# Product 3 of the result in seven block products, batches 2 to 5

## The chip, the core and the metric

The kernel runs on one core of a Trainium2 chip. The metric is the device time in microseconds (us) of one execution. Its engines run side by side, each through its own list of instructions in order: TensorE (PE; PEld is its weight load), VectorE (DVE), ScalarE (ACT) and GpSimd (POOL). Transfers (DMA) are issued from the lists of SyncE (SP) and of POOL; those that add to what lies at their target are issued from POOL. TensorE writes into eight banks of PSUM of 128 x 512 float32 each; VectorE and ScalarE bring results from there to SBUF.

## What is computed

Cross attention over eight batches in float32, `x` and `ctx` of 512 channels and 1024 positions each:

```python
q = einsum('bcn,dc->bnd', x1, Wq) + bq          # d = 64
k = einsum('bcn,dc->bdn', x2, Wk) + bk[:, None]
v = einsum('bcn,dc->bdn', x2, Wv) + bv[:, None]
attn = softmax(einsum('bnd,bdm->bnm', q, k), axis=2)
out = einsum('bcm,bnm->bcn', v, attn) + x1
```

## The kernel before

The value weights are applied last: first y = x2 times the exponentials, then the result o = Wv times y, divided by the sums and with bv and x1 added. Both matrix products are made by a scheme of seven products of half-size blocks in place of eight (numbered 1 to 7 in the table MULT), with sums of blocks on the left and on the right (S1 to S4, T1 to T4) that VectorE makes. The results run through chains: product 1 alone, 1+6, 1+6+5 and so on are grown in the same PSUM bank, and copied out where two results part.

Many of the seven are themselves made in seven block products of 256 columns ("inner" products; `inner_product`, L591). For the result, a block product is one matmul of 128 x 128 by 128 x 256, since its inner blocks have one slice of 128; a plain product of two slices and two rows of blocks is four matmuls of 512 columns.

`period(s, n, nn, nnn)` (L1154) writes out the order by hand for the end of batch s and the start of batch n = s + 1, whose scores and exponentials are made while s is finished. `s.six` is true for batches 2 to 5: in these, product 6 of y is an inner one too. The end of a period is what matters here:

- `multiply_57` (L714) makes products 5, 7 and 3 of the result. 5 and 3 are plain and grow in the bank pair a (after 1 and 6); 7 is an inner one in the pair c. ScalarE's copies of its chain and two exponentials of batch n stand between (the hooks). `complete` adds the third part to the second bank on VectorE.
- `evict_o(s, "22")` reads the pair c, then `second(4)` grows product 4 in it, and `evict_o(s, "21")` reads it again.
- `evict_o(s, "12")` copies the pair a with the bias into the tile r12 (tag "r", ScalarE). Its transfers, x1 added from DRAM and the result written, are kept as `n.leave` and issued in the next period, after `complete_1`.
- Between them POOL issues `sum_t3` (two transfers that add e tiles), `add_11(n, "S3")`, and `total_0(n)`: a VectorE sum over the blocks of the exponentials of half 0, an all-reduce over the partitions, and a small transfer "fews" that lays the sums over partitions.
- The next period (s and n move up by one) makes products 1, 2 and 6 of y, with `total_1` (sum 1 on VectorE, its all-reduce on POOL), `evict_y(s, "11")` from the pair c, `invert(s, 0)` (VectorE adds and inverts fews) and then the left sums of product 7 from S3. The scores of the next batch use the pair c for their second tile.

Tiles share SBUF by tags: a tile waits until its tag's last holder has been read for the last time (with bufs=2, the holder before that). The tag "fold" holds maxima and sums, with two buffers; "y22" holds y22 and, in batches 2 to 5, the copy u1 of product 1 of y; "aI3" holds block sums.

Batch 7 (`multiply_573`, L631) makes product 3 in seven block products already, with 5, 7 and 4, in an order of its own; its left sums of w_S4 are made in its period (`left_values("o3", "S4")`, L1505). In batches 0 and 1 sum 0 of batch 1 is made by three adding transfers (`add_tile`) onto a copied tile (`copy_first`).

Of the kernel before, what the change touches and what calls it, by code (L numbers as in the profile page):

```python
# [15 lines left out]
def kernel(  # L16
# [48 lines left out]
    P = 128  # L65
# [211 lines left out]

    def total_0(s):

        s.mx[0] = f = sb.tile([P, 2, H], F32, tag="fold", name=f"sum_{s.b}_0", bufs=2)  # L280
        x, y = (s.inner[i, "m"].rearrange("q z k (p f) -> q z k p f", p=D) for i in (1, 2))
        nc.vector.tensor_tensor(f.rearrange("q k (p z f) -> q z k p f", p=D, z=2), x, y, ALU.add)
        fold_halves(s, 0, ALU.add)
        s.den[0] = sb.tile([P, H], F32, tag="den", name=f"den_{s.b}_0", bufs=2)
        nc.gpsimd.partition_all_reduce(s.den[0], f[:, 0, :], P, ReduceOp.add)  # L285
        s.few[0] = sb.tile([D, 2, H // P], F32, tag="fews", name=f"fews_{s.b}", bufs=2)
        nc.gpsimd.dma_start(
            s.few[0].rearrange("p z f -> p (z f)"), s.den[0][0:1, :].rearrange("o (p f) -> o p f", p=D)
        )

    def sum_1(s):

        t = s.t["T3"]
        s.mx[1] = sb.tile([P, 2, H], F32, tag="fold", name=f"sum_{s.b}_1", bufs=2)
        nc.vector.tensor_tensor(s.mx[1], t[:, 0:2, :], t[:, 2:4, :], ALU.add)
        fold_halves(s, 1, ALU.add)

# [12 lines left out]
    def invert(s, h):  # L310

        few = s.few[h]
        s.row[h] = row = dram.tile([1, H], F32, tag="row", name=f"row_{s.b}_{h}")
        to = row.rearrange("o (p f) -> (o p) f", p=P)
        if h == 0 and s.b > 1:
            nc.vector.tensor_tensor(few[:, 0, :], few[:, 0, :], few[:, 1, :], ALU.add)
# [296 lines left out]
    def left_values(i, k):  # L613

        x = w[k]
        inner_w[i] = v = {f"{p + 1}{q + 1}": x[:, q : q + 1, ts(p, P)] for p in range(2) for q in range(2)}
        if i == "o3":
            sums = sb.tile([P, 4, 1, P], F32, tag="aS1", name=f"w_I{k}")
        else:
            sums = const.tile([P, 4, 1, P], F32, name=f"w_I{k}")  # L620
# [10 lines left out]
    def multiply_573(s):  # L631
# [33 lines left out]
        for x in ORDER573:  # L665
# [15 lines left out]
            elif x[0] == 4:  # L681
                part, k = divmod(x[1], 2)
                if x[1] == 2:
                    s.bank["last"] = last = ps_a.tile([P, H], F32, tag="c0", name="ps_last")
                if x[1] == 0:
                    last_left(s, True)
                    evict_o(s, "12", rows=(0,))
                ps, j, n = ((a[0], 0, slice(0, H)), (last, 1, left), (a[1], 1, right))[part]
                nc.tensor.matmul(
                    ps[:, n],  # L690
                    w["22"][:, k, ts(j, P)],
                    s.y["T4"][:, k, n],
                    start=part == 1 and k == 0,
                    stop=k == 1,
                    skip_group_check=True,
                )
            else:
                i, z = f"o{x[0]}", x[1]
                ps, opens, copies = steps[x]
                inner_product(s, i, z, ps, opens)  # L700
                for o, of in copies:
                    copy(o, of)
                if x == (7, 7):
                    add_v("22", v7)
                    add_v("21", v7)
                elif x == (3, 1):
                    add_v("12", v3)
                elif x == (7, 3):
                    evict_o(s, "22")
                elif x == (3, 5):  # L710
                    evict_o(s, "12", rows=(1,))
                    last_left(s)

    def multiply_57(s, hook):  # L714

# [233 lines left out]
    def evict_o(s, k, hook=None, rows=range(2)):  # L949
# [18 lines left out]
        if add is None:  # L968
            o = sb.tile([P, 2, H], F32, tag="u1" if k == "11" else "r", name=f"r{k}_{s.b}")
            for j in range(2):  # L970
                nc.scalar.activation(o[:, j, :], s.bank[bank, j], AF.Identity, bias=bias(j))  # L971
                if hook:
                    hook(j)
        else:
            u = s.tmp[add]
            o = sb.tile([P, 2, H], F32, tag="y12", name=f"o{k}_{s.b}") if k == "21" else u
# [32 lines left out]
    def copy_first(s, h):  # L1009

        s.mx[h] = sb.tile([P, 2, H], F32, tag="fold", name=f"sum_{s.b}_{h}", bufs=2)
        nc.scalar.copy(s.mx[h], s.e[h][:, :, 0, :])

    def sums(s, h):
        for i in range(1, MH):
            fold(s, h, i, "sum", ALU.add)
        total(s, h)

    def head_queries(s, x_sb, h, n, bank=None):

# [31 lines left out]
    def head(s):  # L1052
# [36 lines left out]
        s.mx[0] = f = sb.tile([P, 2, H], F32, tag="fold", name=f"max_{s.b}_0", bufs=2)  # L1089
# [64 lines left out]
    def period(s, n, nn, nnn):  # L1154
# [278 lines left out]
                sum_y(s, "T1")  # L1433
        hooks = {}
        if s.b == 0:
            hooks = {6: lambda: exponential(n, 0, 1), 4: lambda: copy_first(n, 0)}
# [31 lines left out]
        if five:  # L1468
            if nn is None:
                scale_y(s, "22")  # L1470
            sum_y(s, "T1")
            weave(
                in_turn(lowers(n, 0, 2 + s.six, MH), lowers(n, 1, 0, 2)),
                sums_o7,
            )
        if s.b == 0:
            add_tile(n, 0, 1)
            sum_y(s, "T4")
        if n is None:
            sum_y(s, "T4")  # L1480
# [3 lines left out]
        if s.b == 0:  # L1484
            exponentials(n, 0, 2)
            lower(n, 0, 3)
            add_tile(n, 0, 2)
# [13 lines left out]
        else:  # L1501
            nc.gpsimd.dma_start(s.x[:, 2:4, 0:H], s.tmp[6], accum_op=ALU.add)
        second(2)
        if n is None:
            weave(left_values("o3", "S4"))  # L1505
        evict_o(s, "11", while_11 if n else None)
        if s.b == 0:
            add_tile(n, 0, 3)
            add_x1(s, "21")
        if n:  # L1510
            if five:
# [43 lines left out]
        if n:  # L1555
# [6 lines left out]
                left_stream(n, 2, n.a["12"], "aI3" if n.b > 1 else "aS4"),  # L1562
            )
            last = evict_o(s, "12")
            if five:
                negate(n, "S3")
                add_11(n, "S3")
            n.leave = [last] if five else [leave, last]
            second(4)
            if five:  # L1570
                total_0(n)
            else:
                total(n, 0)
            evict_o(s, "21")
        else:
            finish(s)
# [43 lines left out]
```

## Time and profile before

| | us |
|---|---|
| median of three runs | 665.11 (664.92 to 665.66) |
| the profiled execution | 665.49 |
| its span from first to last instruction | 663.5 |
| TensorE busy, share of the span | 658.6, 99% |
| VectorE busy | 625.3, 94% |
| ScalarE busy | 379.0, 57% |
| POOL busy | 208.9, 31% |

The profile is of one execution. A row of the timeline gives start, duration, engine, line, operation, `out<-in` by the program's names (batch numbers left out), shapes and count, and in brackets the idle time ahead of it and what ended it. Rows of the list of waits give total, times and longest. Rows of transfers give count, size and the time from issue to landing. Line numbers are those of the kernel before unless said otherwise.

### The profile page before, as it was taken

What the parts mean: (1) busy time and instruction counts of PE and PEld (TensorE: products, weight loads), DVE (VectorE), ACT (ScalarE), POOL (GpSimd) and SP (SyncE); (2) the same over time, 40 slices, a digit from 0 to 9 for tenths busy, and PEclk for the clock granted to TensorE, in tenths of its full rate; (3) what the DMA queues carried; (4) which work ended last, traced back from release to release, by engine and by line L of the source; (5) the groups of instructions that cost most, each with busy time, mean ns of one, the idle gap of its engine ahead of it and who ended that gap; (6) DMA issues with size and microseconds to landing.
All of it is one profiled execution on the core that took longest, in us unless ns stands there. A gap on an engine that the chain in (4) does not pass through costs nothing.

```text
span 663.5 us, 8006 instructions
## 1 busy us (share of the span) xinstructions
PE 658.6 (99%) x2626; PEld 434.2 (65%) x2626; DVE 625.3 (94%) x890; ACT 379.0 (57%) x727; POOL 208.9 (31%) x179
## 2 busy tenths in 40 slices
PE   9999999999999999999999999999999999999997
PEld 5435755756658666677666686576865757666865
DVE  1999999999999999999999999999999999999997
ACT  3755457446475575665766646756567446474332
POOL 0125215631335402363034430354212640224300
PEclk9999999999999999999999999999999999999999
DMA  8687578994789759897598895987928995368614
GB/s 326 261 271 256 124 250 150 212 259 144 261 170 223 190 161 282 177 232 192 145 285 175 206 239 161 250 178 182 277 50 197 217 204 175 78 128 183 121 40 150
DMA packets 47368, 129.05 MB, mean 195 GB/s; under 512 B 5472, under 2 KB 5984, under 8 KB 47328
## 3 DMA queue, kind: packets, MB, share of 16 engines
q0 software_dynamic: 20336, 55.12, 45.8%
q1 hardware_dynamic: 26848, 73.29, 30.4%
q8 instruction: 21, 0.34, 0.2%
q14 instruction: 19, 0.16, 0.1%
q10 hardware_dynamic: 144, 0.14, 0.1%
HBM read 87.83 MB, written 16.81 MB: 158 GB/s over the span
## 4 chain that ended last, share of the span: by engine, by line
PE 94%; DVE 5%; issue 1%; ACT 0%
PE ps_yc L596 9%; PE ps_ya L596 7%; PE ps_oc L485 7%; PE ps_oa L730 6%; PE ps_s L236 6%; PE ps_ya L485 4%; PE ps_q L191 4%; PE ps_oa L485 4%; PE ps_i5chain L596 3%; PE ps_k L191 3%; PE ps_i7chain L596 3%; PE ps_i4b L881 3%; PE ps_i1chain L596 3%; PE ps_i2chain L596 3%; PE ps_i3chain L596 3%; PE ps_oc L881 2%
## 5 line engine op out<-in xcount | busy, mean ns | idle before, releaser
L340 DVE TENSOR_TENSOR e<-e,top 128x1024 f32<-128x1024 f32 x60 | 72.1, 1217 | 0.2 <-POOL top L272 0.2
L349 ACT ACTIVATE e<-e 128x1024 f32<-128x1024 f32 x60 | 62.8, 1058 | 15.9 <-DVE e L340 15.5
L272 POOL PARTITION_ALL_REDUCE top<-max x16 | 32.1, 2008 | 103.6 <-DVE max L266 44.2
L245 ACT COPY e<-ps_s 128x512 f32<-128x512 f32 x90 | 47.7, 619 | 10.2 <-PE ps_s L236 10.2
L304 POOL PARTITION_ALL_REDUCE den<-sum x10 | 33.4, 3337 | 43.2 <-DVE sum L266 38.3
L236 PE MATMUL ps_s<-q,k 64*128 64x512 f32 (+1 forms) x188 | 46.6, 598 | 0.0
L256 DVE TENSOR_TENSOR max<-max,e 128x1024 f32<-128x1024 f32 x30 | 36.5, 1218 | 0.3
L236 PEld LDWEIGHTS ps_s<-q,k 64*128 64x128 f32 x188 | 17.5, 186 | 19.9 <-issue 16.9
L916 DVE TENSOR_TENSOR y<-y,den 128x1024 f32<-128x1024 f32 x24 | 29.2, 1220 | 0.3
L787 ACT COPY ps_yc<-ps_i7chain 128x256 f32<-128x256 f32 x32 | 11.4, 357 | 30.2 <-PE ps_i7chain L596 25.6
L787 ACT COPY ps_ya<-ps_i1chain 128x256 f32<-128x256 f32 x28 | 10.0, 357 | 31.6 <-PE ps_i1chain L596 28.1
L730 PE MATMUL ps_oa<-yT,w_S 128*128 128x512 f32 x56 | 27.5, 592 | 0.0
L285 POOL PARTITION_ALL_REDUCE den<-sum x6 | 19.4, 3229 | 25.3 <-DVE sum L266 25.3
L730 PE MATMUL ps_oa<-y,w_S 128*128 128x512 f32 x56 | 26.3, 592 | 0.0
L325 POOL DMA_DIRECT2D den<-row x12 | 6.7, 561 | 60.0 <-DMA row<-few 36.6
L191 PE MATMUL ps_q<-x_in_x_dram,wqk_sb 128*64 128x512 f32 x112 | 25.6, 598 | 0.0
L485 PE MATMUL ps_oc<-yT,w 128*128 128x512 f32 x56 | 25.3, 594 | 0.1
L787 ACT COPY ps_ya<-ps_i5chain 128x256 f32<-128x256 f32 x32 | 11.5, 360 | 24.1 <-PE ps_i5chain L596 20.0
L485 PE MATMUL ps_oa<-yT,w_S 128*128 128x512 f32 x56 | 25.2, 593 | 0.0
L550 DVE TENSOR_TENSOR aI<-a 128x256 f32<-128x256 f32 x60 | 24.7, 411 | 0.0
L596 PE MATMUL ps_yc<-e,aI 128*128 128x256 f32 x92 | 23.6, 379 | 0.0
L983 POOL DMA_DIRECT2D r<-in_x_dram x14 | 18.3, 1309 | 15.9 <-ACT r L971 15.9
(358 smaller groups left out, 1861.3 us busy)
## 6 DMA issues: line engine op xcount, KB each, us to landing
x_in_x_dram<-in_x_dram SPq DMA_DIRECT2D x60, 512.0 KB, 7.5
a<-in_x2T_dram SPq DMA_DIRECT2D x32, 512.0 KB, 5.7
aS<-in_x2T_dram POOLq DMA_DIRECT2D x21, 512.0 KB, 5.7
eT<-eT POOLq DMA_DIRECT2D x16, 512.0 KB, 11.8
r<-in_x_dram POOLq DMA_DIRECT2D x14, 512.0 KB, 7.1
uo<-in_x_dram POOLq DMA_DIRECT2D x14, 512.0 KB, 8.8
out_dram<-r SPq DMA_DIRECT2D x14, 512.0 KB, 3.3
e<-e POOLq DMA_DIRECT2D x13, 512.0 KB, 7.1
```

The costliest lines, as they stand in the source:

```text
L191: nc.tensor.matmul(ps[r, :], w_sb[:, c, :], s.x[:, c, ts(h, H)], start=(c == 0), stop=(c == CT - 1),)
L236: nc.tensor.matmul(ps[g][:, n], s.k[r, ts(i, P)], s.q[r, ts(h, H)][:, n], start=True, stop=True)
L245: nc.scalar.copy(e[:, g, i, :], ps[g])
L256: nc.vector.tensor_tensor(f, e[:, :, 0, :] if i == 1 else f, e[:, :, i, :], op)
L304: nc.gpsimd.partition_all_reduce(s.den[h], s.mx[h][:, 0, :], P, ReduceOp.add)
L340: nc.vector.tensor_tensor(e, e, top, ALU.subtract)
L349: nc.scalar.activation(e, e, AF.Exp)
L485: nc.tensor.matmul(ps, left[ka][:, k, ts(j, P)], right[kb][:, k, :], start=opens and k == 0, stop=i in (2, 3, 4) and k == n_k - 1, skip_gr ...
L596: nc.tensor.matmul(ps, s.inner[i][ka][:, k, :], s.inner[i, "t"][kb][:, k, :], start=opens and k == 0, stop=z in (2, 3, 4) and k == n_k - 1 ...
L730: nc.tensor.matmul(ps, w[ka][:, k, ts(j, P)], s.y[kb][:, k, :], start=False, stop=i == 3 and k == 1, skip_group_check=True,)
L787: nc.scalar.copy(out, of)
L881: nc.tensor.matmul(ps, s.inner[i][ka][:, k, :], s.inner[i, "t"][kb][:, k, :], start=opens and k == 0, stop=z in (2, 3, 4) and k == n_k - 1 ...
```

## The change

In batches 2 to 5 `multiply_all_573` takes the place of `multiply_57`: product 3 is made in seven block products in a bank pair d of its own (from the four banks of the tag "s"), woven with 5 and 7 by the table ORDER_573. The pair d needs the same copies as any chain (four of 128 x 256 by ScalarE, one of them the third part v3). After `evict_o(s, "12")`, `join_3` copies the pair d into a tile of the tag "y22" (two copies of 128 x 512 by ScalarE) and adds it to r12 by a transfer, then v3 to the second row of r12 by another. VectorE makes the right sums of product 3 (three operations per batch, in the tag "aI3").

Besides, "fold" has one buffer now; the first sum of batch 0 takes the tag "u6"; the left sums of w_S4 are made once, in batch 1, and kept; sum 0 of batch 1 comes from `total_0` in place of the three transfers and the copied first tile.

```diff
@@ fold, total_0, sum_1, head
-            s.mx[h] = sb.tile([P, 2, H], F32, tag="fold", name=f"{kind}_{s.b}_{h}", bufs=2)
+            tag = "u6" if (kind, s.b, h) == ("sum", 0, 0) else "fold"
+            s.mx[h] = sb.tile([P, 2, H], F32, tag=tag, name=f"{kind}_{s.b}_{h}")
...
+    ORDER_573 = (
+        (5, 0), (5, 1), (7, 1), (7, 7), (5, 2), (7, 6), (3, 7), (3, 1), (7, 2),
+        (7, 5), (3, 6), (5, 3), (7, 4), (7, 3), (3, 5), (3, 2), (3, 4), (3, 3),
+    )
+
+    def multiply_all_573(s, hook):
...
+        c0, c1 = (ps_a.tile([P, H], F32, tag=f"c{j}", name=f"ps_oc{j}_{s.b}_7") for j in range(2))
+        chain, third = inner_parts(s, "o7")
+        d0, d1 = (ps_s.tile([P, H], F32, tag="s", name=f"ps_od{j}_{s.b}_3") for j in range(2))
...
+            (3, 7): (d1[:, left], True, []),
+            (3, 1): (d1[:, right], False, [(d0[:, left], d1[:, right]), (v3, d1[:, left])]),
+            (3, 6): (d1[:, right], False, [(d1[:, left], d1[:, right])]),
+            (3, 2): (d0[:, left], False, []),
+            (3, 5): (d1[:, right], False, [(d0[:, right], d1[:, right])]),
+            (3, 4): (d1[:, left], False, []),
+            (3, 3): (d0[:, right], False, []),
...
+    def join_3(s):
+
+        t = sb.tile([P, 2, H], F32, tag="y22", name=f"uo3_{s.b}")
+        for j in range(2):
+            nc.scalar.copy(t[:, j, :], s.bank["d", j])
+        nc.gpsimd.dma_start(s.r12, t, accum_op=ALU.add)
+        nc.gpsimd.dma_start(
+            s.r12[:, 1, :].rearrange("p (a n) -> p a n", a=2),
+            s.third.unsqueeze(1).to_broadcast([P, 2, H // 2]),
+            accum_op=ALU.add,
+        )
...
-    def add_tile(s, h, i):
-        nc.gpsimd.dma_start(s.mx[h], s.e[h][:, :, i, :], accum_op=ALU.add)
...
             fold(n, 1, 3, "max", ALU.max)
+            if s.six:
+                sums_o3 = right_stream(s, "o3", s.y["22"], "aI3")
+                next(sums_o3)
...
-                in_turn(lowers(n, 0, 2 + s.six, MH), lowers(n, 1, 0, 2)),
-                sums_o7,
+                in_turn(
+                    lowers(n, 0, 2 + s.six, MH),
+                    left_values("o3", "S4") if s.b == 1 else (),
+                    lowers(n, 1, 0, 2),
+                ),
+                in_turn(sums_o7, sums_o3 if s.six else ()),
...
-            complete_7 = multiply_57(s, while_57)
+            if s.six:
+                complete_7 = multiply_all_573(s, while_57)
+            else:
+                complete_7 = multiply_57(s, while_57)
...
             last = evict_o(s, "12")
+            if s.six:
+                join_3(s)
...
-            if five:
-                total_0(n)
-            else:
-                total(n, 0)
+            total_0(n)
```

The order of TensorE at the end of batch 3. Names: oa is the pair a (products 5 and 3 before), oc the pair c (product 7), io7 its chain and third part, od the pair d; w_S4 and w_IS4 are the left blocks of product 3, y22 and eIo3 the right ones. Before, from the third matmul of product 5 on:

```order
L730 MATMUL ps_oa1_3_1_2231<-yT1_3_2217,w_S1_74 128x512
L596 MATMUL ps_io7chain_3_2319<-eIo7eT1_3_2265,w_I21_565 128x256
L596 MATMUL ps_oc0_3_7_2317<-yT3_3_2160,w_21_72 128x256
L730 MATMUL ps_oa1_3_1_2231<-yT1_3_2217,w_S1_74 128x512
L596 MATMUL ps_io7chain_3_2319<-eIo7eT1_3_2265,w_I21_565 128x256
L596 MATMUL ps_oc1_3_7_2318<-eIo7eT1_3_2265,w_21_72 128x256
L730 MATMUL ps_oa0_3_1_2230<-y22_3_2152,w_S4_76 128x512
L596 MATMUL ps_oc0_3_7_2317<-yT3_3_2160,w_I21_565 128x256
L730 MATMUL ps_oa0_3_1_2230<-y22_3_2152,w_S4_76 128x512
L730 MATMUL ps_oa1_3_1_2231<-y22_3_2152,w_S4_76 128x512 x2
```

And with the change, from the first block product of product 3 on:

```order
L597 MATMUL ps_od1_3_3_2347<-eIo3aI3_3_2245,w_IS4_1211 128x256
L597 MATMUL ps_od1_3_3_2347<-y22_3_2173,w_S4_76 128x256
L597 MATMUL ps_oc0_3_7_2342<-yT3_3_2181,w_21_72 128x256
L597 MATMUL ps_io7chain_3_2344<-eIo7eT1_3_2288,w_I21_565 128x256
L597 MATMUL ps_od1_3_3_2347<-eIo3aI3_3_2245,w_IS4_1211 128x256
L747 MATMUL ps_oa1_3_1_2254<-yT1_3_2238,w_S1_74 128x512
L597 MATMUL ps_oc1_3_7_2343<-eIo7eT1_3_2288,w_21_72 128x256
L597 MATMUL ps_oc0_3_7_2342<-yT3_3_2181,w_I21_565 128x256
L597 MATMUL ps_od1_3_3_2347<-eIo3aI3_3_2245,w_IS4_1211 128x256
L597 MATMUL ps_od0_3_3_2346<-y22_3_2173,w_S4_76 128x256
L597 MATMUL ps_od1_3_3_2347<-eIo3aI3_3_2245,w_S4_76 128x256
L597 MATMUL ps_od0_3_3_2346<-y22_3_2173,w_IS4_1211 128x256
```

The four matmuls of 512 columns on y22 are gone; seven of 256 into od0 and od1 stand between those of 5 and 7, and the last four of them, (3,5), (3,2), (3,4) and (3,3), stand together at the end.

The order of POOL at the same place, from the addition of x1 to uo5 on (a21 is S3 of batch 4, den and sum belong to its sum 0, r12 is the tile of result block 12 of batch 3). Before:

```order
L983 DMA uo5_3_2322<-in_x1_dram 128x2x512
L181 DMA a21_4_1739<-in_x2T_dram 128x1024
L285 ISA den_4_0_2391<-sum_4_0_2388 128x512
L287 DMA fews_4_2393<-den_4_0_2391 64x1x8
L983 DMA r12_3_2379<-in_x1_dram 128x2x512
L160 DMA aS4_4_2421<-in_x2T_dram 128x1024
```

With the change:

```order
L1050 DMA uo5_3_2349<-in_x1_dram 128x2x512
L772 DMA r12_3_2413<-uo3_3_2416 128x1024
L773 DMA r12_3_2413<-vo73_3_2348 128x2x256
L181 DMA a21_4_1744<-in_x2T_dram 128x1024
L286 ISA den_4_0_2430<-sum_4_0_2427 128x512
L288 DMA fews_4_2432<-den_4_0_2430 64x1x8
L1050 DMA r12_3_2413<-in_x1_dram 128x2x512
L160 DMA aS4_4_2460<-in_x2T_dram 128x1024
```

Two transfers into r12 stand ahead of S3's, of the all-reduce of sum 0 and of everything behind it.

More of the change, by code (lines that the diff above doesn't have):

```diff
@@ L278, in total_0 @@
     def total_0(s):
-        s.mx[0] = f = sb.tile([P, 2, H], F32, tag="fold", name=f"sum_{s.b}_0", bufs=2)
+        s.mx[0] = f = sb.tile([P, 2, H], F32, tag="fold", name=f"sum_{s.b}_0")
         x, y = (s.inner[i, "m"].rearrange("q z k (p f) -> q z k p f", p=D) for i in (1, 2))
@@ L293, in sum_1 @@
         t = s.t["T3"]
-        s.mx[1] = sb.tile([P, 2, H], F32, tag="fold", name=f"sum_{s.b}_1", bufs=2)
+        s.mx[1] = sb.tile([P, 2, H], F32, tag="fold", name=f"sum_{s.b}_1")
         nc.vector.tensor_tensor(s.mx[1], t[:, 0:2, :], t[:, 2:4, :], ALU.add)
@@ L314, in invert @@
         to = row.rearrange("o (p f) -> (o p) f", p=P)
-        if h == 0 and s.b > 1:
+        if h == 0 and s.b:
             nc.vector.tensor_tensor(few[:, 0, :], few[:, 0, :], few[:, 1, :], ALU.add)
@@ L616, in left_values @@
         inner_w[i] = v = {f"{p + 1}{q + 1}": x[:, q : q + 1, ts(p, P)] for p in range(2) for q in range(2)}
-        if i == "o3":
-            sums = sb.tile([P, 4, 1, P], F32, tag="aS1", name=f"w_I{k}")
-        else:
-            sums = const.tile([P, 4, 1, P], F32, name=f"w_I{k}")
+        sums = const.tile([P, 4, 1, P], F32, name=f"w_I{k}")
         for z, (k, x, y, op) in enumerate(LEFT):
@@ L973, in evict_o @@
                     hook(j)
+            if k == "12":
+                s.r12 = o
         else:
@@ L1004, in finish @@
             nc.sync.dma_start(out[s.b, ts(2 + j, P), n], o)
-    def add_tile(s, h, i):
-        nc.gpsimd.dma_start(s.mx[h], s.e[h][:, :, i, :], accum_op=ALU.add)
[L1009 to L1017, printed above, removed]
     def head_queries(s, x_sb, h, n, bank=None):
@@ L1088, in head @@
         more_keys(0, 1)
-        s.mx[0] = f = sb.tile([P, 2, H], F32, tag="fold", name=f"max_{s.b}_0", bufs=2)
+        s.mx[0] = f = sb.tile([P, 2, H], F32, tag="fold", name=f"max_{s.b}_0")
         copies = [scores(s, 0, i) for i in range(2)]
```

43 lines of the change are left out of this document (36 added, 7 removed).

## The prediction

> **What bounds the kernel now.** I read the page first, then the waits of TensorE, then the timeline of each engine around one batch boundary (batch 3 ends, batch 4 starts, 343 to 405 us).
>
> ```profile
> span 663.5 us, 8006 instructions
> ...
> PE 658.6 (99%) x2626; PEld 434.2 (65%) x2626; DVE 625.3 (94%) x890; ACT 379.0 (57%) x727; POOL 208.9 (31%) x179
> ...
> PE ps_oc L485 <- DVE y L916: 0.2, 1, 0.2
> ```
>
> TensorE is busy all the time and waits once for 0.2 us after its start, so it sets the end. But VectorE stands right behind it at 94%: whatever makes VectorE late by more than its small lead becomes a wait of TensorE. So two questions decide: what TensorE saves, and what the new transfers do to VectorE.
>
> **What TensorE saves.**
>
> ```profile
> 345.61 0.59 PE L596 MATMUL ps_io7chain<-yT,w 128*128 128x256 f32 x2
> 346.04 0.59 PE L596 MATMUL ps_io7third<-eIo7eT,w_I 128*128 128x256 f32 x2
> 346.48 1.02 PE L730 MATMUL ps_oa<-yT,w_S 128*128 128x512 f32 x2
> 347.33 0.59 PE L596 MATMUL ps_io7chain<-eIo7eT,w_I 128*128 128x256 f32 x2
> ```
>
> A program matmul is two instructions. From start to start one of 256 columns takes 346.04 - 345.61 = 0.43 us, one of 512 takes 347.33 - 346.48 = 0.85. Product 3 was 4 of 512 (3.42) and becomes 7 of 256 (3.02): 0.40 us less per batch, 1.6 for four.
>
> Inside the new weave one wait looks uncovered. Block product (3,5) is followed by (3,2), which writes the left half of bank d0, while ScalarE copies (3,5) into its right half. Batch 7 already runs such a weave:
>
> ```profile
> 651.59 0.38 ACT L702 COPY vo<-ps_od 128x256 f32<-128x256 f32 x1
> ...
> 652.02 0.30 PEld L596 LDWEIGHTS ps_od<-eIo3eT,w_IS 128*128 128x128 f32 x2 [0.28 <-ACT vo L702]
> ...
> 655.57 0.59 PE L596 MATMUL ps_od<-eIo3eT,w_IS 128*128 128x256 f32 x2
> ...
> 656.21 0.36 ACT L702 COPY ps_od<-ps_od 128x256 f32<-128x256 f32 x1 [1.37 <-PE ps_od L596]
> ```
>
> At 652.02 TensorE waited for a copy of the other half of the same bank, so a bank is guarded as a whole. The copy begins 0.64 after (3,5) and takes 0.36, TensorE follows 0.05 later: (3,2) starts 1.05 after (3,5) and not 0.43, +0.62. Bounds: 0 if nothing waits, 0.62 if the copy is prompt; I take 0.62. TensorE then gains -0.40 + 0.62 = +0.2 per batch: the gain is gone before any transfer.
>
> **When the first joining transfer lands.** ScalarE gets four new copies of 128x256 inside the weave and, after r12 (L971 r), two of 128x512 into the new tile. Only then can the first joining transfer, new tile into r12, be issued.
>
> ```profile
> 350.39 2.01 ACT L349 ACTIVATE e<-e 128x1024 f32<-128x1024 f32 x2
> 352.29 1.04 ACT L177 ACTIVATE aS<-aS 128x1024 f32<-128x1024 f32 x1
> 353.24 1.43 ACT L971 ACTIVATE r<-ps_oa,wqk_sb 128x512 f32<-128x512 f32 x2
> ...
> 353.64 0.88 POOL L181 DMA_DIRECT2D aS<-in_x2T_dram  x1 [7.37 <-ACT aS L177]
> 354.51 1.76 POOL L384 DMA_DIRECT2D e<-e  x2
> ...
> 356.63 1.81 POOL L181 DMA_DIRECT2D a<-in_x2T_dram  x1
> 362.73 3.23 POOL L285 PARTITION_ALL_REDUCE den<-sum  x1 [4.29 <-DVE sum L266]
> 366.26 0.56 POOL L287 DMA_DIRECT2D fews<-den  x1 [0.30 <-POOL den L285]
> ...
> aS<-in_x2T_dram POOLq DMA_DIRECT2D x1, 512.0 KB, 5.4
> ...
> a<-in_x2T_dram POOLq DMA_DIRECT2D x1, 512.0 KB, 13.4
> ...
> DMA to landing us min/median/max: 4.6/7.1/9.4
> ```
>
> The last three rows are times from issue to landing. Five accumulating transfers of 512 KB leave POOL from 353.64 to 356.63 (aS, two of e, one of uo, a) and land one behind the other, the first at 359.0, the fifth (a, which is S3 of the next batch) at 370.0: the queue works them off at (370.0 - 359.0) / 4, some 2.7 us each. The joining transfer now is the fifth. By the instruction times above (3,5) has four matmuls of 512 columns and ten of 256 ahead of it, 7.7 us behind the weave's start (343.9, two of 512 ahead of 345.61); its copy starts 0.64 later, the last of the weave, and the two exponentials follow near 352.6 instead of 350.39. The whole train, headed by aS, is 2.2 us late. Landing: 370.0 + 2.2 = **372.2**. The bounds are its issue, near 358.0 (352.6, then 1.9, 0.9, 1.3 and 1.1 for exponentials, aS, r and the two copies), plus the shortest landing of such a transfer inside the chip (4.6, last row, e<-e): 362.6; and one more place in the queue: 374.9. I take 372.2, because it stands where S3 stood.
>
> [...]
>
> **What waits behind it.** The second joining transfer adds into the same tile, so it must wait for the first one's landing, and POOL's instructions stand still while one waits:
>
> ```profile
> POOL den L325 <- DMA row<-few: 36.6, 4, 10.5
> ...
> 370.79 1.21 DVE L295 TENSOR_TENSOR sum<-e 128x1024 f32<-128x1024 f32 x1
> ...
> 373.24 1.28 DVE L932 TENSOR_TENSOR y<-ps_yc,uy 128x512 f32<-128x512 f32 x2
> 374.44 0.64 DVE L316 TENSOR_TENSOR fews<-fews 64x4 f32<-64x4 f32 x1
> ...
> fews<-den POOLq DMA_DIRECT2D x1, 2.0 KB, 4.0
> ```
>
> The first row shows POOL idle for up to 10.5 us before an issue that waits for a landing. Behind the second joining transfer stand the issue of S3, the all-reduce of sum 0, the fews transfer, the x1 addition to r12 and aS4. At 372.2 POOL issues two transfers (0.88 each, 1.76 for two), then runs the all-reduce (3.23): it ends at 377.2 and not at 366.0. The fold tile has one buffer now, so VectorE may write sum 1 (370.79 before) only then: +6.4. It would reach fews at 374.44 + 6.4 = 380.8; fews lands at 377.2 + 0.3 + 4.0 = 381.5, so VectorE is **7.0 us late** from there on. S3, needed right behind, is issued near 374; with the 7.1 of a middling landing it is there by 382.
>
> ScalarE is held too: the new tile lives in y22, and the next copy of product 1 into that tag waits for 372.2. That is shorter than VectorE's delay and goes inside it.
>
> **What of the 7.0 reaches TensorE.**
>
> ```profile
> 334.60 0.70 DVE L874 TENSOR_TENSOR ps_oc<-ps_oc,v 128x512 f32<-128x512 f32 x1 [0.99 <-ACT ps_oc L890]
> ...
> 336.87 0.70 DVE L874 TENSOR_TENSOR ps_i4b<-ps_i4b,v 128x512 f32<-128x512 f32 x1 [0.38 <-ACT ps_i4b L890]
> ...
> 338.93 1.22 DVE L916 TENSOR_TENSOR y<-y,den 128x1024 f32<-128x1024 f32 x1
> ...
> 340.46 3.60 PE L485 MATMUL ps_oc<-y,w 128*128 128x512 f32 x8
> ...
> 376.40 1.02 PE L236 MATMUL ps_sc<-q,k 64*128 64x512 f32 x4
> ...
> 433.98 0.88 POOL L181 DMA_DIRECT2D aS<-in_x2T_dram  x1 [7.37 <-ACT aS L177]
> ```
>
> TensorE feels it first at 376.40: these scores go into the bank that VectorE empties into y at 373.24, now at 379.6 to 380.3 for the first half, near +3.9. The rest of the delay stays in VectorE until TensorE meets it again. The boundaries repeat every 433.98 - 353.64 = 80.34 us (last row), so the rows of 334 to 340 stand for those one period on. Until the y of product 2 (338.93) VectorE's largest idle times are 0.99 and 0.38, 1.4 in all, and the first of the three new operations for product 3 (128x512, some 0.6) eats part of that: y comes 7.0 - 1.4 + 0.6 = 6.2 late, and it was ready only 340.46 - 340.15 = 0.3 ahead of its matmul. So **+5.9 per boundary**, for the three that end batches 2, 3 and 4: 17.7. This is counted against the old schedule, so the +0.2 of the weave lies inside it.
>
> At the fourth (end of batch 5) y22 goes to the third part of product 2 of batch 6:
>
> ```profile
> 525.88 0.37 ACT L787 COPY v<-ps_i2third 128x256 f32<-128x256 f32 x1 [0.51 <-PE ps_i2third L596]
> ...
> 527.40 1.03 PE L596 MATMUL ps_i2chain<-eI2eT,aI 128*128 128x256 f32 x4
> ```
>
> Two periods on from 372.2 that copy waits for 532.9, the next copy ends 0.65 later, and the block of 527.40 starts at 533.6: +6.2.
>
> **The first two batches.** Sum 0 of batch 0 moves to the tag u6, so ScalarE's copy of product 6, into the same tag, waits until the all-reduce has read the sum:
>
> ```profile
> 51.24 3.23 POOL L304 PARTITION_ALL_REDUCE den<-sum  x1 [2.65 <-DVE sum L266]
> ...
> 54.41 1.88 PE L236 MATMUL ps_s<-q,k 64*128 64x512 f32 x8
> ...
> 126.06 2.35 DVE L358 TENSOR_TENSOR eT<-eT,e 128x1024 f32<-128x1024 f32 x2
> ...
> 127.43 7.05 PE L485 MATMUL ps_ya<-eT,aS 128*128 128x512 f32 x16
> ...
> 360.68 1.23 DVE L282 TENSOR_TENSOR sum<-eI1yT,eI2eT 128x1024 f32<-128x1024 f32 x1
> ```
>
> That copy starts at 54.5; four copies at some 0.5 us later the bank that the last scores need (55.3) is free at 56.3: +1.0. In batch 1 VectorE makes a sum of 1.23 (last row's kind) that transfers made before; T2's first half, ready at 127.2 for the matmul of 127.43, comes near 128.4: +1.0. With TensorE already late the second is partly covered: 1.5 for both (0 to 2). The four sums of w_S4, moved from batch 7 to batch 1, stood at the end beside a busy TensorE and stand beside one again; the four transfers and the copy taken out of batch 0 were waited for by nobody. I count both at nothing.
>
> **Sum.** 17.7 + 6.2 + 1.5 = 25.4 us on the profiled execution. That took 665.49 us (span 663.5), 0.4 above the median of 665.11; on the median the forecast is **690 us**.
>
> **Rivals.**
> - The transfer lands some 3 us sooner, at 369.2, because it stays inside the chip. Then sum 1 is 3.4 late, fews 4.1, TensorE 4.1 - 1.4 + 0.6 - 0.3 = 3.0: 3 x 3.0 + 3.2 + 1.5 = 13.7, **679 us**. For it: the first of the five lands 5.4 after its issue. Against: each later one does so more slowly.
> - S3, now behind both joining transfers and beside two result transfers, lands at 385 instead of 382: VectorE waits there 3.5 longer at each boundary, 25.4 + 14, **704 us**. For it: two 512 KB results leave in just these microseconds.
> - The joining transfer lands near 362.6 and nothing behind POOL is late. It decides below 365.8: 365.8 + 1.76 + 3.23 is 370.79, when VectorE asks for the fold tile. What is left is TensorE's own account: from -1.6 (copies covered, start absorbed), **663.5 us**, to +0.9 + 1.5, 667.5. The change does what it says in this case. Against: the 13.4 above.
>
> **Chances.** Forecast 0.60, sooner 0.20, later 0.12, hidden 0.08 (half of it faster). Less than 0.2% (1.3 us) can't be told from no change here. So slower 0.94, same 0.02, faster 0.04. The forecast's own range is 682 to 698; the range that reaches into the neighbours is 674 to 702.
>
> **What would show it.** In the changed kernel (its own line numbers) POOL should show an idle time of some 13 us between the two joining issues, an all-reduce of sum 0 that ends 11 us later after the weave, VectorE waiting for POOL at L296 and for fews at L317, ScalarE waiting for a transfer at L395, and TensorE waiting for VectorE at the scores of bank c and for ScalarE inside the weave at L597 (some 0.6). If the first joining transfer lands within 9 us of its issue, or sum 1 starts without a wait for POOL, the forecast is wrong.

## The result and the profile after

The changed kernel takes 696.65 us (median of 6 runs, 695.59 to 697.08), the kernel before beside it 665.64: 1.0465 times as long, 95% interval 1.0452 to 1.0479. The loss is 31.0 us.

The page of the changed kernel, and its list of waits (total, times, longest; all in us):

```profile
span 694.9 us, 8118 instructions
...
PE 669.1 (96%) x2650; PEld 441.4 (64%) x2650; DVE 631.3 (91%) x904; ACT 386.4 (56%) x750; POOL 214.0 (31%) x184
```

```profile
POOL r L773 <- DMA r<-uo: 46.6, 4, 12.2
...
DVE sum L296 <- POOL den L286: 24.4, 4, 6.4
...
ACT uy L395 <- DMA r<-uo: 10.3, 3, 3.5
...
ACT v L852 <- DMA r<-uo: 7.7, 1, 7.7
...
PE ps_i2chain L597 <- ACT ps_yc L852: 6.7, 2, 6.2
...
PE ps_i6chain L597 <- ACT ps_ya L852: 6.2, 3, 2.1
...
PE ps_sc L236 <- DVE y L997: 3.2, 2, 1.8
...
PE ps_od L597 <- ACT ps_od L756: 1.8, 4, 0.4
```

The busy times of VectorE and ScalarE hardly grew (625.3 to 631.3, 379.0 to 386.4). What is new are waits, and they form a line: POOL waits for the first joining transfer four times, VectorE for POOL four times, ScalarE for the same landing four times, and TensorE for both.

One boundary, batch 3 to 4, in the timeline of the changed kernel. TensorE starts batch 4 here 9.29 us later than before (366.51 against 357.22), so subtract that to compare with the rows that the prediction shows.

```profile
367.13 2.45 POOL L772 DMA_DIRECT2D r<-uo  x1
...
380.92 0.58 ACT L395 COPY uy<-ps_ya 128x512 f32<-128x512 f32 x1 [3.50 <-DMA r<-uo]
381.14 1.20 POOL L773 DMA_DIRECT2D r<-vo  x1 [11.55 <-DMA r<-uo]
...
382.46 4.04 POOL L286 PARTITION_ALL_REDUCE den<-sum  x1
...
382.62 1.30 PE L597 MATMUL ps_i6chain<-eI6y,aI 128*128 128x256 f32 x4 [2.14 <-ACT ps_ya L852]
...
383.72 1.91 PE L597 MATMUL ps_ya<-eT,aS 128*128 128x256 f32 x4
...
386.53 1.23 DVE L296 TENSOR_TENSOR sum<-e 128x1024 f32<-128x1024 f32 x1 [5.98 <-POOL den L286]
...
386.80 0.56 POOL L288 DMA_DIRECT2D fews<-den  x1 [0.30 <-POOL den L286]
...
390.19 1.55 DVE L317 TENSOR_TENSOR fews<-fews 64x4 f32<-64x4 f32 x1
```

The reader should see one landing, near 380.9, that releases two engines within 0.3 us: ScalarE at 380.92 and POOL at 381.14. POOL's all-reduce, behind the second joining transfer, then releases VectorE at 386.53.

How far TensorE lies behind the kernel before tells where the 31 us went. It is read at the first matmul of product 1 of y of each batch, and once at that of product 2 of the result, ahead of the first weave (differences of such rows in the two timelines):

| stretch | changed kernel | e2 (no joining) |
|---|---|---|
| start, batches 0 and 1, up to the weave of batch 2 | 2.42 | 2.45 |
| weave of batch 2 | 0.45 | 0.45 |
| batch 2 to 3, with the next weave | 6.42 | 0.62 |
| batch 3 to 4 | 6.23 | 0.63 |
| batch 4 to 5 | 6.61 | 0.63 |
| batch 5 to 6 | 8.93 | -0.02 |
| sum | 31.06 | 4.76 |

Nothing is lost after that. The last boundary costs most:

```profile
548.67 1.03 PE L597 MATMUL ps_yc<-e,a 128*128 128x256 f32 x4
...
555.17 0.37 ACT L852 COPY v<-ps_i2third 128x256 f32<-128x256 f32 x1 [7.67 <-DMA r<-uo]
...
555.87 2.07 PE L597 MATMUL ps_i2chain<-eI2eT,aI 128*128 128x256 f32 x4 [6.17 <-ACT ps_yc L852]
...
557.74 1.91 PE L597 MATMUL ps_yc<-eI2eT,a 128*128 128x256 f32 x4
...
559.44 1.77 PE L597 MATMUL ps_yc<-e,aI 128*128 128x256 f32 x4
...
561.05 4.46 PE L486 MATMUL ps_ya<-eT,aS 128*128 128x512 f32 x10
```

A block of four such matmuls takes 0.86 from start to start (547.81 to 548.67 just ahead). The three after the stop take 1.87, 1.70 and 1.61: 2.6 us more. The windows (length, then busy time and count of each engine, granted clock, share and rate of DMA) give the reason:

```profile
543.50:549.50 6.00, 6.00 (x29) 5.13 (x27) 5.93 (x9) 2.04 (x4) 0.00 (x0) 1.00 1.06 190
...
555.80:562.00 6.20, 6.13 (x15) 4.64 (x16) 1.22 (x1) 3.19 (x7) 5.90 (x5) 0.58 0.88 166
562.00:568.00 6.00, 6.00 (x15) 2.38 (x13) 5.92 (x11) 1.03 (x2) 5.70 (x5) 1.00 0.81 131
```

After the stop the granted clock is 0.58 on average over 6.2 us, and 1.00 ahead of it and behind. So the 8.93 are 6.34 of stop (555.87 against 549.53, when the block would have started) and 2.6 of slow clock. TensorE's wait here is of 6.17 us; the last section has shorter ones that a lower clock followed.

### The profile page after: what moved, and what is told of

Same layout as the page of the kernel before. It is cut to its first block, busy times and chain, and to the rows that moved or that the text cites. A ratio compares the mean times of both kernels' runs of the same rounds, so it can differ in the third digit from the quotient of the medians.

```text
span 694.9 us, 8118 instructions
## 1 busy us (share of the span) xinstructions
PE 669.1 (96%) x2650; PEld 441.4 (64%) x2650; DVE 631.3 (91%) x904; ACT 386.4 (56%) x750; POOL 214.0 (31%) x184
## 4 chain that ended last, share of the span: by engine, by line
PE 45%; DVE 27%; issue 11%; DMA 10%; POOL 6%; ACT 1%; SPq 0%; POOLq 0%; DVEq 0%; ACTq 0%
DMA r<-uo 8%; PE ps_yc L597 5%; DVE e L341 3%; DVE max L257 3%; DVE aI L551 3%; PE ps_s L236 3%; PE ps_ya L486 3%; PE ps_ya L597 3%; PE ps_k L191 2%; PE ps_i5chain L597 2%; PE ps_oc L486 2%; PE ps_i7chain L597 2%; PE ps_i4b L946 2%; PE ps_i3chain L597 2%; PE ps_oa L795 2%
## 5 line engine op out<-in xcount | busy, mean ns | idle before, releaser
L236 PE MATMUL ps_s<-q,k 64*128 64x512 f32 (+1 forms) x188 | 49.1, 599 | 0.1
L305 POOL PARTITION_ALL_REDUCE den<-sum x9 | 33.3, 3704 | 20.4 <-DVE sum L267 15.5
L286 POOL PARTITION_ALL_REDUCE den<-sum x7 | 25.4, 3634 | 21.2 <-DVE sum L267 21.2
L296 DVE TENSOR_TENSOR sum<-e 128x1024 f32<-128x1024 f32 x8 | 9.8, 1221 | 24.4 <-POOL den L286 24.4
L236 PEld LDWEIGHTS ps_s<-q,k 64*128 64x128 f32 x188 | 19.4, 186 | 19.3 <-issue 15.2
L486 PE MATMUL ps_oa<-yT,w_S 128*128 128x512 f32 x56 | 25.2, 593 | 0.0
L181 POOL DMA_DIRECT2D aS<-in_x2T_dram x7 | 7.2, 1030 | 52.8 <-ACT aS L177 52.8
L486 PE MATMUL ps_oc<-y,w 128*128 128x512 f32 x48 | 22.0, 601 | 0.9 <-DVE y L981 0.9
L257 DVE TENSOR_TENSOR max<-e 128x1024 f32<-128x1024 f32 x15 | 18.3, 1219 | 5.0 <-POOL den L305 3.1
```

Source lines behind the costliest of these rows:

```text
L236: nc.tensor.matmul(ps[g][:, n], s.k[r, ts(i, P)], s.q[r, ts(h, H)][:, n], start=True, stop=True)
L305: nc.gpsimd.partition_all_reduce(s.den[h], s.mx[h][:, 0, :], P, ReduceOp.add)
L486: nc.tensor.matmul(ps, left[ka][:, k, ts(j, P)], right[kb][:, k, :], start=opens and k == 0, stop=i in (2, 3, 4) and k == n_k - 1, skip_gr ...
```

## The experiments

**e1: the other edits alone.**

```diff
-            if s.six:
-                complete_7 = multiply_all_573(s, while_57)
-            else:
-                complete_7 = multiply_57(s, while_57)
+            complete_7 = multiply_57(s, while_57)
...
-            if s.six:
-                join_3(s)
...
```

VectorE's right sums of product 3 are left out with it.

> The changed kernel with product 3 of batches 2 to 5 left in its old form (plain, in bank pair a) and no joining transfers; the other edits stay (one fold buffer, u6 for the first sum, sum 0 of batch 1 on VectorE, the sums of w_S4 made in batch 1). Theory (the loss of batches 2 to 5 comes from POOL standing still between the two joining transfers): only the 2.4 us that the start and batches 0 and 1 lost between the two profiles remain, 668.0 (667 to 669). Rival (the single fold buffer costs something at every boundary, without any joining transfer): 672 or more.

Measured: 668.04, 1.0036 times before (1.0026 to 1.0046). The other edits cost 2.45 us, all of it by batch 2 (TensorE's lag is 2.51 there and stays so for six batches). One fold buffer costs nothing at a boundary as long as POOL is on time.

**e2: no joining.**

```diff
             last = evict_o(s, "12")
-            if s.six:
-                join_3(s)
```

> The changed kernel without joining: product 3 is made in seven block products but its bank pair is neither copied nor added, so product 3 is missing from result block 12 of batches 2 to 5. Theory: TensorE's own account is left, 668.0 for the start and some 0.5 per batch for the weave (the rise of TensorE's lag across the weave in the profiles): 670 (669 to 672). Rival (VectorE's three added operations for product 3, 0.69 + 0.42 + 0.42 = 1.5 us per batch at 91% busy, are what is paid): 668 + 4 x 1.5 = 674 or more.

Measured: 670.41, 1.0064 times before (1.0047 to 1.0081). VectorE's three added operations are nearly hidden: the table has 0.63 per period in this kernel, 0.45 of it in the weave, so 0.18 is left for them and all else. 696.65 - 670.41 = 26.2 us belong to the joining. TensorE's own account is a loss of 0.45 over each weave, and its rows say why (changed kernel, weave of batch 5):

```profile
531.91 0.70 PE L597 MATMUL ps_od<-eIo3aI,w_IS 128*128 128x256 f32 x2
...
532.45 1.02 PE L747 MATMUL ps_oa<-yT,w_S 128*128 128x512 f32 x2
...
534.17 0.59 PE L597 MATMUL ps_od<-eIo3aI,w_IS 128*128 128x256 f32 x2
...
535.21 0.70 PE L597 MATMUL ps_od<-y,w_S 128*128 128x256 f32 x2 [0.45 <-ACT ps_od L756]
...
535.75 0.59 PE L597 MATMUL ps_od<-eIo3aI,w_S 128*128 128x256 f32 x2
```

From (3,5) to (3,2) 1.04 us pass instead of 0.43. Two blocks more take 0.54 instead of 0.43. That is -0.40 + 0.61 + 0.22 = +0.43.

**e3: the second joining transfer behind sum 0.**

```diff
...
             total_0(n)
+            if s.six:
+                join_third(s)
             evict_o(s, "21")
```

(`join_third` holds the second of `join_3`'s two transfers.)

> The changed kernel with the second joining transfer (third part) moved behind the all-reduce of sum 0 and the fews transfer on POOL; every transfer is still made. Theory: the all-reduce ends near its old time, VectorE's sum 1 waits for nothing, the three boundaries after batches 2, 3 and 4 cost some 0.5 to 2 instead of 6.4; the one after batch 5 keeps its loss, since ScalarE's copy there waits for the landing of the first joining transfer (9.5): 668 + 3 x 1.0 + 9.5 = 680 (676 to 684). Rival (the added transfers themselves, by their traffic beside S3 and the result transfers, make the others late, wherever POOL waits): 690 or more.

Measured: 692.45 (1.0376 to 1.0421 times before). The first half of the expectation came: VectorE's sum 1 waits for nothing. The second did not: the time is on the rival's side, but the rows show a wait and not traffic. From the boundary that the rows above show:

```profile
379.41 1.21 DVE L296 TENSOR_TENSOR sum<-e 128x1024 f32<-128x1024 f32 x1
379.75 0.58 ACT L395 COPY uy<-ps_ya 128x512 f32<-128x512 f32 x1 [3.75 <-DMA r<-uo]
...
381.45 1.93 PE L597 MATMUL ps_i6chain<-eI6y,aI 128*128 128x256 f32 x4 [2.39 <-ACT ps_ya L855]
...
383.17 1.91 PE L597 MATMUL ps_ya<-eT,aS 128*128 128x256 f32 x4
```

ScalarE's copy into y22 waits for the landing, the copies for product 6 stand behind it, and TensorE waits for those (2.39), and then the granted clock is 0.53 on average over the 3.60 us from 381.40 on (1.00 over the 2.40 ahead). With that hold alone the three boundaries cost 5.2, 4.9 and 4.8 and the last 8.5, where e2 has 0.6 and nothing.

**e4: sum 0 in another tag (y11).**

```diff
-        s.mx[0] = f = sb.tile([P, 2, H], F32, tag="fold", name=f"sum_{s.b}_0")
+        s.mx[0] = f = sb.tile([P, 2, H], F32, tag="y11" if 2 < s.b < 7 else "fold", name=f"sum_{s.b}_0")
```

> The changed kernel with sum 0 of batches 3 to 6 in the tag y11 in place of fold, so that VectorE's sum 1 has not to wait until the all-reduce of sum 0 has read it. Theory: POOL is as late as before, so VectorE starts sum 1 some 6 us earlier but then waits at y of bank c (same tag y11) and for fews, which lands as late as before; the loss stays, 696 (693 to 698). Rival (the single fold buffer is the cause and 4 KB more would mend it): three or four boundaries lose their 6.4 us wait, 671 to 678.

Measured: 748.69. Neither. Its list of waits begins with:

```profile
ACT v L852 <- POOL den L286: 74.1, 4, 18.9
```

The tag y11 also holds the third part of product 1 of y, which ScalarE copies early in the next period, so the edit made a wait of its own. It decides nothing about the fold tile; e12 does.

**e5: the tag of the copied pair alone.**

```diff
-        t = sb.tile([P, 2, H], F32, tag="y22", name=f"uo3_{s.b}")
+        t = sb.tile([P, 2, H], F32, tag="yT4", name=f"uo3_{s.b}")
```

> The changed kernel with the copy of bank pair d (the source of the first joining transfer) in the tag yT4 in place of y22, so that ScalarE's copies of the next period have not to wait for the landing; both joining transfers stay where they are on POOL. Theory now (two holds stand side by side at each boundary, VectorE's by POOL and ScalarE's by the tag, and either alone costs nearly as much): POOL and VectorE's sum 1 are as late as before, three boundaries keep 5 to 6 us; the one after batch 5 loses its long stop and goes from 9.0 to 6 or less: 670.4 + 3 x 5.5 + 5 = 692 (686 to 695). Rival (the hold on ScalarE is what stops TensorE, and VectorE's wait lies inside it): 672 to 677.

Measured: 695.62 (693.74 to 697.17), just above the range that was expected.

```profile
POOL r L773 <- DMA r<-uo: 45.7, 4, 11.8
...
DVE sum L296 <- POOL den L286: 23.6, 4, 6.3
...
PE ps_sc L236 <- DVE y L997: 10.8, 4, 3.2
```

ScalarE's waits for the landing are gone, TensorE now waits for VectorE at the scores of bank c. The first three boundaries cost 7.0, 7.9 and 6.9, as much as with both holds or more; the last fell from 8.9 to 5.1. Some 0.9 of each is the edit's own: product 4 still reads yT4, so ScalarE's copy into it waits 1.06 (367.34) and TensorE 0.67 behind that copy, at product 1 of y (369.69). Even without the 0.9 the three cost 6.0 to 7.0. So either hold is enough for the three, and at the last the tag was worth 3.8.

**e6: both holds taken away** (the edits of e3 and e5).

> Both holds taken away: the second joining transfer behind the all-reduce of sum 0 and fews, and the tag yT4. All transfers are still made. Theory (two holds side by side): what is left is the kernel without joining, 670.4, and a little where POOL waits for the landings behind fews: 671 to 675. Rival (a third cause, such as S3 or the result transfers being late by the traffic): 680 or more.

Measured: 688.67 (685.33 to 690.54). The rival's side of the line, but not its traffic:

```profile
DVE max L257 <- POOL den L305: 17.6, 5, 5.0
...
ACT v L855 <- DMA out_dram<-r: 12.6, 3, 5.1
...
PE ps_i5chain L597 <- ACT ps_ya L855: 8.2, 3, 3.7
```

r12 is now added to three times, one after the other (pair d, third part, x1), and then written out. The tag "r" goes next to the third part of product 5 of y, and ScalarE's copy into it waits 5.1 us for that writing. POOL, standing still for two landings behind fews, makes the all-reduce of sum 1 late as well. A third hold was behind the first two. The trace shows it as waits one behind the other; whether traffic made these landings longer as well was not tried apart, and the 0.9 per boundary that yT4 brings by itself (e5) is in this time too.

**e7 and e9: one joining transfer.** VectorE adds the third part on the way out of bank d1, and a single transfer (from the tag yT4) is left. e9 does the addition four operations of product 1's right sums later.

```diff
+    def add_third(s):
...
+        s.third_sum = t = sb.tile([P, 2, H], F32, tag="yT4", name=f"uo3_{s.b}")
+        halves = [x.rearrange("p (a n) -> p a n", a=2) for x in (s.third_sum[:, 1, :], s.bank["d", 1])]
+        nc.vector.tensor_tensor(*halves, s.third.unsqueeze(1).to_broadcast([P, 2, H // 2]), ALU.add)
...
+        t = s.third_sum
+        nc.scalar.copy(t[:, 0, :], s.bank["d", 0])
         nc.gpsimd.dma_start(s.r12, t, accum_op=ALU.add)
...
```

> The third part is added by VectorE on the way out of bank d1 (one operation of 128x512 per batch, in place of a copy by ScalarE), so one joining transfer is left, in tag yT4, in its place on POOL. Theory: nothing on POOL waits before fews, both holds are gone, VectorE has about 0.7 us more work per batch and 1 to 2 us of idle time to put it in: 671 to 674. Rival (VectorE sets the pace once the holds are gone): 670.4 + 4 x 0.7 and more, 674 or above.

Measured: 677.56, the rival's number, but its list of waits shows another reason:

```profile
DVE uo L771 <- PE ps_oc L486: 6.3, 4, 1.6
```

VectorE stood waiting for product 4, which still read yT4.

> As e7_one_yt4, with VectorE's addition of the third part four operations of product 1's right sums later, so that product 4, which reads the tag yT4, is done by then. Theory (of the 7.1 us that e7 lost against the kernel without joining, 6.3 are VectorE's wait there, 1.6 per batch): 677.6 - 6.3 = 671.3 (670.5 to 672.5). Rival (VectorE's own 0.7 us more per batch, and what POOL does behind, is the loss): 675 to 678.

Measured: 671.90 (1.0092 times before, 1.0075 to 1.0108). The wait was the difference. With one transfer that nothing on POOL waits for ahead of fews, joining costs some 1.5 us (671.90 - 670.41, two sets of runs) in place of 26.2.

**e8: joining by VectorE, no transfer.** r12 is read from bank pair a by VectorE together with the copied pair d, and earlier than before, ahead of `leave()`. The copy lies in the tag y22.

```diff
+                if k == "12" and s.six:
+                    u = s.third_sum[:, j, :]
+                    nc.vector.scalar_tensor_tensor(o[:, j, :], s.bank[bank, j], bias(j), u, ALU.add, ALU.add)
+                    continue
...
```

> No joining transfer at all: VectorE adds the third part (0.7 us) and reads bank pair a with the bias and the copied product 3 into r12 (2 x 0.7), in place of ScalarE's read. VectorE has some 2.1 us more per batch. Theory (VectorE's idle time of some 1.8 us per batch in the kernel without joining takes most of it): 671 to 674. Rival (VectorE is the bound, its work goes to the time in full): 670.4 + 4 x 2.1 = 679.

Measured: 676.69, between the two. Of 2.1 us more per batch on VectorE, (676.69 - 670.41) / 4 = 1.6 came out in the time, so VectorE has only some 0.5 us of room per batch at this place. The trace shows the way it takes: VectorE's operation o reads bank c late, ScalarE's copy into that bank waits for it, and TensorE for the copy, 1.3 of the 1.6.

```profile
371.20 1.40 DVE L1044 SCALAR_TENSOR_TENSOR o<-ps_oc,wqk_sb,uo 128x512 f32<-128x512 f32 x2
372.03 0.36 ACT L847 COPY ps_yc<-ps_i2chain 128x256 f32<-128x256 f32 x1 [2.13 <-DVE o L1044]
...
372.44 1.13 PE L597 MATMUL ps_i2chain<-eI2eT,aI 128*128 128x256 f32 x4 [1.31 <-ACT ps_yc L847]
```

The 1.6 is still a quarter of what the transfers cost, 26.2 / 4 = 6.6.

**e10: another block between (3,5) and (3,2).**

```diff
-        (7, 5), (3, 6), (5, 3), (7, 4), (7, 3), (3, 5), (3, 2), (3, 4), (3, 3),
+        (7, 5), (3, 6), (5, 3), (7, 4), (3, 5), (7, 3), (3, 2), (3, 4), (3, 3),
```

> As e9_one_later, with (7,3) put between (3,5) and (3,2) in the weave of products 5, 7 and 3, so that TensorE has 0.43 us of work while ScalarE copies (3,5) out of the same bank. Theory (the wait for the bank, 0.6 from start to start, is paid in full by TensorE): 4 x 0.43 = 1.7 us less than e9. Rival (VectorE or ScalarE sets the end of this stretch, TensorE's wait is covered by them): the same as e9 within 0.4.

Measured: 671.34, 0.6 less than e9 and neither of the two expected numbers, with intervals that overlap. The wait for the bank is gone from the list, and TensorE's lag over a weave falls from 0.45 to 0.02; but over the rest of the period it rises from 0.44 to 0.82. The gain in the weave is real, and most of it is given back behind it. The trace shows where: 0.44 stand at product 1 of y in both kernels (the wait that yT4 brings, as in e5), and 0.37 are new, at product 2 of y, by the way that e8 shows: VectorE, ScalarE, TensorE.

```profile
367.59 1.40 DVE L1045 SCALAR_TENSOR_TENSOR o<-ps_oc,wqk_sb,uo 128x512 f32<-128x512 f32 x2
...
368.42 0.36 ACT L852 COPY ps_yc<-ps_i2chain 128x256 f32<-128x256 f32 x1 [0.92 <-DVE o L1045]
...
368.83 0.73 PEld L597 LDWEIGHTS ps_i2chain<-eI2eT,aI 128*128 128x128 f32 x4 [0.51 <-ACT ps_yc L852]
```

**e11: the first joining transfer one place earlier.**

```diff
             if s.six:
                 join_3(s)
+                leave()
```

(and `leave()`, the addition of x1 to uo5, no longer ahead of it)

> The changed kernel with the addition of x1 to uo5 (and the writing of that result) issued behind the two joining transfers, so that the first joining transfer is the fourth of its train on POOL and not the fifth. Nothing else is moved. Theory (its landing is set by its place in the queue, some 2.7 us for each): it lands about 11.0 after its issue and not 13.7, POOL's wait falls to some 9.5, sum 1 waits 2.7 less: each of the four boundaries 2.7 cheaper, 696.65 - 10.8 = 686 (683 to 690). Rival (its landing has nothing to do with the place: the transfer itself takes 13 us): 695 to 698.

Measured: 689.97 (687.70 to 697.68; 1.032 to 1.0442 times before). Time from issue to landing, changed kernel and e11:

```profile
r<-uo POOLq DMA_DIRECT2D x4, 512.0 KB, 13.7
```

```profile
r<-uo POOLq DMA_DIRECT2D x4, 512.0 KB, 11.0
```

One place in the train is worth 2.7 us, as the prediction took from the five transfers of before. The same transfer of 512 KB lands after 13.7 as the fifth and after 11.0 as the fourth, so between these two kernels the landing goes with the place in the queue. The place alone does not fix it: in e9, still behind the same four, it takes 11.8 at the median. The time fell by 6.7 and not by 10.8, and one of the four runs (697.68) did not fall at all. In the profiled run the last boundary gained 5.3, the other three only 1.2, 0.5 and 1.7. The rows of batch 3 to 4 name two reasons: the addition to uo5 now stands between the second joining transfer and the all-reduce, which ends 6.85 behind the landing and not 5.66; and TensorE, no longer stopped by ScalarE, waits 2.67 for VectorE at the scores, and the four instructions of these scores (387.29) then take 2.67, where they took 1.02 before (376.40).

**e12: sum 0 in a tag that is free (yT4).** As e4, with "yT4" for "y11".

> The changed kernel with sum 0 of batches 3 to 6 in the tag yT4, free at that time, so that VectorE's sum 1 need not wait for the all-reduce of sum 0; POOL and the tag y22 are left as they are. Theory (POOL late and ScalarE held by y22, the fold tile only passes the first on): sum 1 is on time, but fews lands as late as before, and ScalarE's copies wait for the landing as before; three boundaries of about 5, and 8.9 after batch 5: 670.4 + 3 x 5 + 8.9 = 694 (689 to 697). Rival (the single fold buffer is the cause): three boundaries lose their 6.2 and the one after batch 5 at least half, 670 to 678.

Measured: 695.66. VectorE's sum 1 starts on time, and the wait has moved to the next place (same boundary):

```profile
380.37 1.21 DVE L296 TENSOR_TENSOR sum<-e 128x1024 f32<-128x1024 f32 x1
...
389.13 2.99 DVE L317 TENSOR_TENSOR fews<-fews 64x4 f32<-64x4 f32 x1 [5.03 <-DMA fews<-den]
```

So the fold tile only passed POOL's lateness on; 4 KB more would not have mended it.

No version tried beats the kernel before: the best, e10, is 1.0085 times as long (1.0069 to 1.0102). Of its 5.2 us, about 2.5 are the other edits.

## Why the prediction was right, and where it was off

- **The landing.** Forecast 372.2 on the old time scale; 367.13 + 13.71 (the transfer's time in the chain of waits) - 9.29 = 371.6. The issue was forecast near 358.0 and came at 357.8. That it goes with the place in the train is shown by e11: 13.7 from issue to landing as the fifth, 11.0 as the fourth.
- **POOL, then VectorE.** The all-reduce was to end at 377.2 and ended at 386.50 - 9.29 = 377.2; sum 1 was to be 6.4 late and waits 6.4, 6.0 in the row shown. That the end fits so well is partly luck: the landing came 0.6 earlier, and the second joining transfer and S3 took 2.4 up to the all-reduce in place of 1.8 (its recorded 4.04 begin while S3's issue still runs, to 383.28). One detail failed: VectorE does not wait for fews. It lands 1.9 after its issue at the median, not 4.0, before VectorE comes. The delay of 7.0 there came about otherwise: 6.5 from sum 1, and 0.9 because the small addition at 390.19 took 1.55 and not 0.64, 7.4 in all.
- **The three boundaries.** Forecast 5.9 each, 17.7; measured 6.42, 6.23 and 6.61, 19.3. The path was not the one described. "That is shorter and goes inside" was right for the sum (e5: without ScalarE's hold the three cost no less), but ScalarE's hold stops TensorE first, and by e3 the three cost nearly 5 with it alone. In the lag, read as for the table, this stop is worth 2.3 at each of the three. At the boundary shown 1.8 of slow clock follow (0.50 granted over 3.41 us), and 0.5 at the scores; at the other two 2.2 to 2.4 of waiting for VectorE at the scores. So TensorE is 4.4 to 4.8 late there, where 3.9 was forecast by VectorE alone. The two holds are alternatives, not a large one and a small one, and the size of 5.9 came out nearly right although about half of the delay at the scores, and at the boundary shown nearly all of it, came by the other way.
- **The step that was mis-sized most: the fourth boundary.** Forecast 6.2, measured 8.93. The stop is 6.34, as worked out; the 2.6 of slow clock behind it (0.58 granted on average over 6.2 us) were missing from the sum, which has no term for the clock at any boundary.
- **The first two batches.** Forecast 1.5, measured 2.4. The first wait stands where it was put: ScalarE's copy of product 6 starts at 54.27 (forecast 54.5; TensorE's lag grows by 0.83). The new sum makes VectorE late in batch 1 (0.97), but only 0.2 of that stand at T2; 0.77 come earlier, at product 2 of y (124.98), where bank c is free late. The second was to be "partly covered" by the first. It was not, and some 0.6 came at other places, 0.4 ahead of these two and 0.2 in batch 2.
- **The weave.** Forecast +0.2, measured +0.43 by the rows and +0.45 in the lag. The wait for the bank was right (1.04 against 1.05 from start to start); the two slower blocks around it were missing. For batch 2 that weave stands ahead of the first boundary and adds 0.45 that the sum did not have.

The differences add up: 2.7 + 1.6 + 0.9 + 0.45 = 5.65, which is 31.06 - 25.4. Of the rivals, "lands sooner" and "hidden" fell with the landing; that a transfer inside the chip lands sooner than one from DRAM was not shown (medians before: 7.1 for e<-e, 5.7 for aS<-in_x2T_dram). S3 is issued at 381.85, and VectorE, late by then, shows no wait for it. e2 and e9 give what the change would have cost without the chain of transfers: 670 to 672, a loss in any case, since the other edits cost 2.45 (e1) and TensorE gained nothing in the weave.

## What to carry to other kernels

- Before a transfer replaces an addition, write down what its tile, its source's tag and its issuing engine hold while it is under way. Here one landing held a queue, a copy tag and a result tile, and taking one hold away showed the next (696.7, 692.5, 688.7). What helped was to have fewer dependent transfers (671.9).
- Price a transfer's landing by the place where it will stand in its queue, read from the same place of the same trace: here one transfer landed after 13.7 us as the fifth of its train and after 11.0 as the fourth.
- When a wait of TensorE is forecast, look at the clock behind it as well: here a stop of 6.3 us cost 2.6 more, and one of 2.1 cost 1.8 more.

## What the runs showed of the hardware that was not expected

- The granted clock fell to half after stops far shorter than the long one. In the changed kernel TensorE's wait of 2.14 us was followed by 3.41 us at 0.50, in e3 one of 2.39 by 0.53 on average over 3.60 us; yet in e12 one of 2.67 left the clock at 1.00. So the length of the wait alone does not decide in these three. The first two rows are the changed kernel, the others e12:

```profile
380.04:383.46 3.42, 1.28 (x7) 0.80 (x6) 0.51 (x2) 1.95 (x5) 2.32 (x3) 1.00 0.90 306
383.46:386.87 3.41, 3.41 (x10) 2.66 (x9) 0.34 (x1) 1.33 (x2) 3.11 (x2) 0.50 0.94 150
```

```profile
378.70:382.11 3.41, 1.63 (x8) 1.10 (x6) 3.38 (x6) 0.81 (x3) 0.59 (x1) 1.00 0.99 317
382.11:385.52 3.41, 2.52 (x12) 2.23 (x13) 1.99 (x4) 2.44 (x6) 3.41 (x3) 1.00 0.89 149
```

The clock record of the changed kernel falls to half at 383.46, 554.12 and 694.07; the second and the third fall lie 50.0 and 91.0 times 3.413 us behind the first, and the stretches at half clock behind the first two take 3.41 and 6.83. The first two windows above are cut at these points. The wait of the changed kernel lies inside one such stretch (3.42 - 1.28 = 2.14 idle); that of e12 is cut in two by the windows set there, 1.78 and 0.89. With the changed kernel cut in this way from its start on, without the last 14 us, a stretch at full clock with 2.14 us or more of idle TensorE was followed by one at half clock (twice: 2.14 ahead of 383.46 and 3.41 ahead of 554.12), and none with 1.72 or less was (1.72 in the one that ends at 468.79). So the idle time within one stretch fits these two kernels where the length of the wait does not. That it decides is the author's reading of these few rows, and what places a wait against the stretches was not shown.

- A 64x4 addition on VectorE took 0.64 before, 1.55 in the changed kernel and 2.99 in e12, and 0.15 where no all-reduce runs on POOL (the last one of each of these traces). In the three longer cases it lies inside an all-reduce, and each time it ends 2.2 to 2.3 us after that all-reduce begins, counted from the end of POOL's issue ahead of it where the two overlap (372.83 before, 389.52, 389.89). So in these three it seems to be held until then, and the earlier it starts ahead of that the longer it takes (0.64, 1.55, 2.99); why was not tried.
